# An RGCN layer with a gate on one core: the middle nine weight matrices taken one outer product at a time, each outer product by seven products of quarters

## The chip, the cores and the metric

The kernel runs on one core of a Trainium2 chip. The metric is the device time of one execution in microseconds (us); lower is better. The time of the kernel before is the median of three runs, 1311.46 us (1311.43 to 1313.43).

## The reference

```
h = maximum(layernorm(x), 0)                      # x: 1250 x 1024, float32
u = h @ root + bias
for r in range(8):                                # 20,000 edges (src, dst, type), sorted by dst
    mask = (edge_type == r)
    sums = segment_sum(h[src] * mask[:, None], dst, 1250)
    mean = sums / maximum(segment_sum(mask, dst, 1250), 1)[:, None]
    u = u + mean @ weight[r]                      # weight: 8 x 1024 x 1024
z = concatenate([u, h], 1) @ w_gate + b_gate      # w_gate: 2048 x 1024
out = x + tanh(u) * z + h * (1 - z)
```

Everything is float32. The mean commutes with the product, so the kernel first makes `h @ weight[r]` for all nodes and then gathers rows of it for the edges.

## The kernel before

**Eleven matrices.** `mats` is the eight `weight[r]`, then `root`, then the lower half of `w_gate` (these ten are multiplied by `h`), then the upper half of `w_gate` (multiplied by `u`). The code counts them s = 0 to 10; "matrix six" in this text is s = 5. The 1250 rows of `h` are ten blocks of 128 rows (`ND`, the last of 98), taken in five pairs (`NP`): pair i is the blocks i and i + 5.

**The outer seven products.** One pair (256 rows) times one matrix (1024 x 1024) is done by the Strassen-Winograd scheme: seven products of a 128x512 operand with a 512x512 operand in place of eight. The seven left operands of all pairs are made once and kept in SBUF (`h_op[i]`, slots `A11, A12, A22, S1, S2, S3, S4`); the seven right operands of a matrix (`Factors`) are made by four VectorE subtractions of 128x2048, `make_t1` to `make_t4`, in nine buffers `wbuf`. One 128x512 operand times one 512x512 operand is four matmuls with 512 moving columns (`KQ` = 4, line L509).

**The inner seven products.** For the matrices s = 1 to 9 the two row blocks of two neighbouring pairs (0 and 1, 2 and 3) are taken together for some of the seven kinds of product, and Strassen-Winograd is applied once more: seven products of quarters with 256 moving columns (two matmuls each, line L253 in `Second.add`) in place of eight. The classes `Second`, `Third`, `First` and `Fifth` do this for A12, S4, A11 and S1. The other three kinds, and all seven kinds of the fifth pair, which has no partner, stay at 512 columns. For s = 8 and 9 `Fifth` serves the first two pairs alone (`fifths`). Each class makes its inner sums on VectorE for each two pairs: four 128x512 differences of the right operand and four 128x256 sums of the left operands (`Third.sums` and `next_sums`, L307 to L316). The four 128x256 sums of the left operands for `Second` are made once, at s = 1, kept in DRAM (`lefts_dram`) and loaded again.

**Order of the work.** `steps` runs over (s, i), matrix outside and pair inside. `step` calls `product` for one pair. `product` issues the seven outer products and, in the places that the dictionary `fill` gives, the inner ones. After each of them it calls `between(j)`, which first issues what the matrix itself needs (loads of the next matrix, `make_t1` and so on, inner sums) and then one or more steps of a generator with side work. Engines run their own queues in order, and buffers and semaphores tie them; so the position in the program decides behind what an instruction stands on its engine.

**Results.** PSUM has eight banks here: four `ps`, two `ps_b` (`lead`), `ps_n` and `ps_q`. Products are copied or added from PSUM into two SBUF tiles `row` of 128x1024, and `put` stores each finished block of 512 KB in one transfer from the SP queue to `y[g]`, `hr_dram` or `z_dram`.

**Side work.** At s = 0 the layer norm and the transposes of `h` go on beside the matmuls. The generator `index()` builds a table of the edges: `scatters()` issues 157 small indirect transfers from GpSimd (`to_table`, L1011), each followed by three `memset` of `apart` (L1019), and advances one step for two of them; `order()` loads the table back (`in_table`, L1260, from the SP queue), counts (`of_nodes`, L1024 and on, VectorE), sends the counts through DRAM to all partitions (`v_bc`, L1265), and ranks the nodes (`larger`, L1034). From s = 5 on, the generator `edges` gathers rows of `y[0]` (matrices s = 0 to 4) for 118 slots of edges, from s = 8 on rows of `y[1]` for 75 slots: `add_slot` issues an indirect gather of 128 rows on GpSimd (L1448) and one 128x1024 multiply-add on VectorE (L1453). `spread` divides the steps evenly over the `between` calls. GpSimd runs ahead of VectorE by the five buffers `got`.

**The end.** The gate product (s = 10) is five calls of `product` with `u` as the left operand, with tanh, the mixing and a scatter of the rows to the output.

A part of `step` that shows how the old order is put together (i = 1):

```
fill = dict(first=lambda: (e.first(), q and q.first(t[1][:, :Q]), 0)[-1],
            fifth=lambda: (e.sixth(), True),
            sixth=lambda: (e.seventh(), e.to_first(to), 0)[-1])
```

## Time and profile before

| | |
|---|---|
| median of three runs | 1311.46 us (1311.43 to 1313.43) |
| the profiled execution's own time | 1308.14 us |
| its span, first to last instruction | 1306.4 us |
| granted TensorE clock | 0.998 |
| busy: TensorE, VectorE, GpSimd, ScalarE | 1290.2, 956.8, 632.2, 285.2 us |
| bytes moved | 263.12 MB, mean 201 GB/s |

The profile shows one execution. A float32 matmul of the program stands in the trace as two MATMUL instructions, so counts of matmul instructions are twice those of the code. A group's "busy" is the union of its instructions' times; durations of pipelined instructions overlap, so the distance from start to start is shorter than one duration. "PEld" is the weight loads, "SP" the engine that issues transfers, "POOL" is GpSimd, "DVE" is VectorE, "ACT" is ScalarE.

### The profile page before, as it was taken

To read this page: it belongs to the slowest core of one execution; us is meant where nothing else is said; L and a number is where in the kernel's file an instruction comes from. 1 tells how busy PE (TensorE), PEld (TensorE's weight loads), DVE (VectorE), ACT (ScalarE), POOL (GpSimd) and SP (SyncE) were. 2 spreads that over 40 slices of the span, in tenths; PEclk is the share of its full clock that TensorE was granted. 3 is DMA by queue.
4 is the path that set the end of the run, shared out by engine and by line. 5 is a ranking of instruction groups with operands and counts; after the bars stand their busy time and mean duration, and the time that the engine had idled before them with its cause. 6 is when DMAs were issued, how large, how long until landed. Compare 5 with 4: busy or idle time off the path is not lost.

```text
span 1306.4 us, 13118 instructions
## 1 busy us (share of the span) xinstructions
PE 1290.2 (99%) x4075; PEld 758.7 (58%) x4075; DVE 956.8 (73%) x1439; ACT 285.2 (22%) x530; POOL 632.2 (48%) x974
## 2 busy tenths in 40 slices
PE   9999999999999999999999999999999999999997
PEld 5344666566566656646665665666566466544443
DVE  7964653553454797458998988998888899867974
ACT  3342222122122212212221221222122112122210
POOL 0046666665664057402454546556265555615632
PEclk9999999999999999999999999999999999999999
DMA  8864113311422362445648779788789958979951
GB/s 316 295 192 154 67 76 123 116 49 56 155 85 74 132 123 62 70 148 188 233 151 333 247 252 361 287 295 305 244 276 336 381 157 269 340 248 304 340 159 60
DMA packets 110306, 263.12 MB, mean 201 GB/s; under 512 B 34424, under 2 KB 36021, under 8 KB 110099
## 3 DMA queue, kind: packets, MB, share of 16 engines
q0 software_dynamic: 44064, 118.20, 28.1%
q1 hardware_dynamic: 50034, 112.03, 24.8%
q10 hardware_dynamic: 16128, 31.98, 7.4%
q8 instruction: 32, 0.52, 0.2%
q14 instruction: 48, 0.39, 0.1%
HBM read 200.74 MB, written 76.42 MB: 212 GB/s over the span
## 4 chain that ended last, share of the span: by engine, by line
PE 46%; issue 5%; POOL 2%; DMA 2%; DVE 1%; ACT 0%; POOLq 0%; DVEq 0%
PE ps_b L509 22%; PE ps L253 11%; PE ps L509 3%; PE ps_n L253 2%; PE ps_b L253 2%; PE ps_q L253 2%; PE ps_q L509 2%; PE ps_n L509 2%; DMA got<-y,idx 2%; POOL out_dram L907 1%; POOL got L901 0%; POOL got L1448 0%; PE ps L452 0%; POOL h_op L901 0%; DVE h_op L490 0%
## 5 line engine op out<-in xcount | busy, mean ns | idle before, releaser
L509 PE MATMUL ps_b<-w,h_op 128*128 128x512 f32 x1464 | 657.1, 593 | 2.2 <-ACT row L617 1.6
L509 PEld LDWEIGHTS ps_b<-w,h_op 128*128 128x128 f32 x1464 | 276.6, 190 | 303.7 <-issue 290.6
L1448 POOL DMA_INDIRECT got<-y,idx x193 | 254.4, 1318 | 267.8 <-DVE u L1453 177.5
L1453 DVE SCALAR_TENSOR_TENSOR u<-got,w_of,u 128x1024 f32<-128x1024 f32 (+1 forms) x193 | 247.1, 1283 | 38.0 <-DMA got<-y,idx 35.5
L1011 POOL DMA_INDIRECT table<-row_col,at_i x157 | 171.3, 1091 | 173.3 <-issue 101.2
L509 PE MATMUL ps<-w,h_op 128*128 128x512 f32 (+1 forms) x296 | 129.7, 581 | 2.5 <-DVE h_op L490 1.9
L253 PE MATMUL ps<-inner 128*128 128x256 f32 x480 | 120.8, 380 | 0.6 <-DVE inner L308 0.4
L253 PEld LDWEIGHTS ps<-inner 128*128 128x128 f32 x480 | 91.1, 190 | 26.6 <-issue 10.6
L509 PEld LDWEIGHTS ps<-w,h_op 128*128 128x128 f32 x296 | 56.0, 190 | 69.7 <-issue 64.1
L253 PE MATMUL ps<-w,h_op 128*128 128x256 f32 x352 | 90.3, 379 | 0.0
L253 PEld LDWEIGHTS ps<-w,h_op 128*128 128x128 f32 x352 | 66.8, 190 | 31.1 <-issue 22.4
L535 ACT COPY row<-ps_b 128x512 f32<-128x512 f32 x53 | 31.0, 585 | 231.0 <-PE ps_b L509 227.2
L617 ACT COPY row<-ps_b 128x512 f32<-128x512 f32 x54 | 31.6, 585 | 220.9 <-PE ps_b L509 220.9
L253 PE MATMUL ps<-w,w 128*128 128x256 f32 x288 | 69.8, 379 | 0.0
L253 PEld LDWEIGHTS ps<-w,w 128*128 128x128 f32 x288 | 54.8, 190 | 15.9 <-issue 9.6
L661 ACT COPY row<-ps_b 128x512 f32<-128x512 f32 x40 | 23.4, 585 | 176.6 <-PE ps_b L509 165.2
L1019 POOL MEMSET apart<- 128x1 f32 x471 | 52.6, 112 | 18.1
L949 POOL DMA_INDIRECT node_dram<-ids,pos_i x20 | 26.4, 1318 | 54.7 <-DVE pos_i L1277 48.9
L509 PE MATMUL ps_q<-w,h_op 128*128 128x512 f32 x112 | 51.8, 592 | 0.0
L570 ACT COPY row<-ps_b 128x512 f32<-128x512 f32 x54 | 31.7, 588 | 82.7 <-PE ps_b L509 78.4
L193 DVE TENSOR_TENSOR w<-w,w 128x2048 f32<-128x2048 f32 (+1 forms) x12 | 25.3, 2112 | 29.0 <-PE ps L509 29.0
L541 DVE TENSOR_TENSOR row<-row 128x512 f32<-128x512 f32 x44 | 30.2, 686 | 20.4 <-ACT row L535 20.3
(232 smaller groups left out, 1536.1 us busy)
## 6 DMA issues: line engine op xcount, KB each, us to landing
y<-row SPq DMA_DIRECT2D x72, 512.0 KB, 4.8
w<-in_L_gnn_weight_dram ACTq DMA_DIRECT2D x21, 1024.0 KB, 10.4
w<-in_L_gnn_weight_dram SPq DMA_DIRECT2D x10, 1024.0 KB
w<-lefts_dram SPq DMA_DIRECT2D x16, 512.0 KB, 4.5
w<-in_L_gnn_w_gate_dram ACTq DMA_DIRECT2D x6, 1024.0 KB, 15.6
h_dram<-h_op SPq DMA_DIRECT2D x9, 512.0 KB, 6.4
u<-in_L_gnn_bias_dram SPq DMA_DIRECT2D x9, 512.0 KB
hr_dram<-row SPq DMA_DIRECT2D x9, 512.0 KB, 6.4
```

The source lines that it names most:

```text
L193: nc.vector.tensor_sub(p["t1"][:, k], p["t3"][:, k], p["b11"][:, k])
L253: nc.tensor.matmul(p, a[:, k, :], b[:, k, :], start=(fresh and k == 0), stop=(k == 1), skip_group_check=True)
L509: nc.tensor.matmul(b[:, at], aop[:, i, k, :], w.of[i][:, k, at], start=(fresh and k == 0), stop=(k == KQ - 1), skip_group_check=True)
L535: nc.scalar.copy(d, b)
L541: nc.vector.tensor_add(c22, c if lone else c22, d)
L570: nc.scalar.copy(c11, b)
L617: nc.scalar.copy(c12, b)
L949: ins = nc.gpsimd.indirect_dma_start(out=node_dram[g][:, :], out_offset=bass.IndirectOffsetOnAxis(ap=pos_i[:, g, d:d + 1], axis=0), in_=id ...
L1011: ins = nc.gpsimd.indirect_dma_start(out=table[:, :], out_offset=bass.IndirectOffsetOnAxis(ap=at_i[:, c:c + 1], axis=0), in_=row_col[:, c: ...
L1019: nc.gpsimd.memset(apart, 0.0)
L1448: nc.gpsimd.indirect_dma_start(out=t[:n], out_offset=None, in_=y[g][:, :], in_offset=bass.IndirectOffsetOnAxis(ap=at[:n, d, k:k + 1], axis=0),
L1453: nc.vector.scalar_tensor_tensor(u[:n], t[:n], w, u[:n], op0=OP.mult, op1=OP.add)
```

## The change

For s = 1 to 9 the order is turned round. `steps` now runs over (s, n), where n is one of the seven kinds of outer product in the order A11, A12, S2, S3, S1, S4, A22, and `kind(m, n, between)` does this kind for all five pairs before the next one begins.

- Pairs 0 and 1 form one inner scheme, pairs 2 and 3 another (u = 0, 1). Both share the right-hand differences, which `inner_sums` now makes once for a kind and not once for each two pairs, and the left-hand sums of both lie in one 128x512 operand.
- All seven kinds go by seven products of quarters for s = 1 to 4. From s = 5 on `REGULAR` names kinds that stay at 512 columns and are chained onto what the banks hold: A12 and S4 for s = 5 to 7; A12, S2, S3 and S4 for s = 8 and 9; A22 too for s = 9. The fifth pair stays at 512 columns (`alone`).
- Left-hand sums are kept in DRAM for all seven kinds at s = 1 and loaded for all of them at s = 2 to 4; later for S3 alone, where it isn't regular; else VectorE makes them.
- The four `ps` banks are held through all nine matrices, one for each of the pairs 0 to 3, and each kind accumulates onto them where the scheme allows. `ps_n` and `ps_q` hold the inner partial products.
- Rows leave as halves of 256 KB: `put` notes a store, and `store_rows` issues it on the SP queue one call later. All weight loads go from the SP queue; before, most went from ScalarE's.
- Each kind has five `between` calls. `spread` weighs them by the kind (`SHARE`).
- `to_table` has one `memset` in place of three. `in_table`, the counts and `v_bc` go by GpSimd's queue and not by SP's. `larger` is one for each call.
- The first pair of the gate is prepared during the last two kinds of s = 9 (`hooks`), with its operands in other slots of `h_op`.

The diff, cut to its core:

```
+    REGULAR = ((1, 5), (1, 2, 3, 5))
+    LOADED = (3,)
+    SHARE = (9, 11, 9, 11, 9, 11, 10)
...
+    ORDER = (A11, A12, S2, S3, S1, S4, A22)
...
+    def regular(s, n):
+        return s >= R0[1] and n in REGULAR[s >= R0[2]] or (s, n) == (LAST, 6)
+    def loaded(s, n):
+        return 1 < s < R0[1] or s >= R0[1] and n in LOADED
...
+    def inner_sums(m, n, second):
...
+        if from_dram:
+            nc.sync.dma_start(lefts[:, both], kept)
+        if second:
+            nc.vector.tensor_sub(t3, b22, b12)
+            nc.vector.tensor_sub(t4, b21, t2)
+            if not from_dram:
+                nc.vector.tensor_sub(s3, a11, a21)
+                nc.vector.tensor_sub(s4, a12, s2)
+        else:
+            nc.vector.tensor_sub(t1, b12, b11)
+            nc.vector.tensor_sub(t2, b22, t1)
+            if not from_dram:
+                nc.vector.tensor_add(s1, a21, a22)
+                nc.vector.tensor_sub(s2, s1, a11)
+        if m.s == 1:
+            nc.sync.dma_start(kept, lefts[:, both])
...
+    def kind(m, n, between):
...
+        if chained:
+            alone(range(KQ))
+            alone_rows()
+            call(0)
+            m.make(n)
+            for j, i in enumerate((0, 2, 1, 3)):
+                add(banks[i], h_op[i][:, ORDER[n]], w, fresh=n not in (1, 5))
+                if i == 2:
+                    to_rows_of(0)
+                if i == 0:
+                    next_sums()
+                call(j + 1)
+            to_rows_of(1)
+            return
+        x = sum_bank("ps_n")
+        xs = [x[:, :H], x[:, H:]]
+        for u in range(2):
+            add(xs[u], h_op[2 * u][:, ORDER[n], 0:2], b11, fresh=u == 0)
+        if s == 1 and n == 0:
+            for b in banks:
+                touch(b)
+        for u in range(2):
+            nc.scalar.copy(banks[2 * u][:, :H], xs[u])
+        inner_sums(m, n, 1)
+        y = sum_bank("ps_q")
+        for u in range(2):
+            add(y[:, u * H:(u + 1) * H], left_sum(0)[:, u], right(0), fresh=u == 0)
+        ys = ys_room[n % 2]
+        nc.scalar.copy(ys, y)
+        call(0)
+        for u in range(2):
+            add(xs[u], left_sum(1)[:, u], right(1))
+        for u in range(2):
+            add(banks[2 * u][:, :H], h_op[2 * u][:, ORDER[n], 2:4], b21)
+        for u in range(2):
+            nc.vector.tensor_add(banks[2 * u][:, H:], xs[u], ys[:, u * H:(u + 1) * H])
+        call(1)
+        alone(range(KQ))
+        alone_rows()
+        m.make(n)
+        call(2)
+        for u in range(2):
+            add(xs[u], left_sum(2)[:, u], right(2))
+        for u in range(2):
+            nc.scalar.copy(banks[2 * u + 1].rearrange("p (a n) -> p a n", a=2),
+                           xs[u][:, None, :].to_broadcast([P, 2, H]))
+        next_sums()
+        call(3)
+        for u in range(2):
+            add(banks[2 * u][:, H:], left_sum(3)[:, u], b22)
+        to_rows_of(0)
+        call(4)
+        for u in range(2):
+            add(banks[2 * u + 1][:, :H], h_op[2 * u + 1][:, ORDER[n], 2:4], right(3))
+        for u in range(2):
+            b = banks[2 * u + 1][:, H:]
+            nc.vector.tensor_add(b, b, ys[:, u * H:(u + 1) * H])
+        to_rows_of(1)
...
+    def beside_kind(m, n, k):
...
+        if k != 0 and s < LAST:
+            return
+        if s < LAST:
+            to = {3: "a", 4: "c", 5: "b", 6: "d"}.get(n)
+            if to:
+                matrix_of(s + 1).load(to)
...
@@ to_table
-        for _ in range(3):
-            nc.gpsimd.memset(apart, 0.0)
+        nc.gpsimd.memset(apart, 0.0)
@@ of_nodes
-        nc.sync.dma_start(val_dram.rearrange("g (p d) -> p g d", p=P), val3)
+        nc.gpsimd.dma_start(val_dram.rearrange("g (p d) -> p g d", p=P), val3)
@@ order
-                for _ in range(7):
-                    yield
                 in_table = sp.tile([P, NHI, SLOTS], I32, name="in_table")
-                nc.sync.dma_start(in_table, table.rearrange("(b p s) o -> p b (s o)", p=P, s=SLOTS))
-                for _ in range(8):
+                nc.gpsimd.dma_start(in_table, table.rearrange("(b p s) o -> p b (s o)", p=P, s=SLOTS))
+                for _ in range(14):
                     yield
                 of_nodes(in_table, sp.tile([P, NHI, SLOTS], F32, name="is_edge"), runs, val, ids_f)
                 v_bc = sp.tile([P, G, KEYS], F32, name="v_bc")
-                nc.sync.dma_start(v_bc.rearrange("p g k -> p (g k)"),
+                nc.gpsimd.dma_start(v_bc.rearrange("p g k -> p (g k)"),
                                   val_dram.rearrange("(o g) k -> o (g k)", o=1)
                                   .to_broadcast([P, G * KEYS]))
                 for _ in range(4):
                     yield
...
-                        if d % 2 or at_call[0] == NP - 1:
-                            yield
+                        yield
```

`alone` is the fifth pair's four matmuls of 512 columns; `alone_rows` and `to_rows_of` copy (ScalarE) or add (VectorE) the banks into the half rows and note the stores; `call(k)` issues stores noted earlier, the weight load of `beside_kind` and the side work.

More of the change, by code (lines that the diff above doesn't have):

```diff
@@ new lines, in quarter_rows, with matrix_of @@
+    def quarter_rows():
+        t = [rows.tile([P, D], F32, name="row") for _ in range(4)]
+        q = [r[:, c:c + Q] for r in t for c in (0, Q)] + [b[:, k] for b in halves
+                                                          for k in range(KQ)]
+        sums_of["rows"] = q[:NP], q[NP:2 * NP], q[2 * NP:3 * NP]
+    matrices = {}
+    def matrix_of(s):
+        if s not in matrices:
+            matrices[s] = Matrix(s, matrices[s - 1].w if s > 1 else None)
+        return matrices[s]
+    stores = []
@@ new lines, in store_rows, with put @@
+    def store_rows(n=None):
+        for _ in range(len(stores) if n is None else n):
+            nc.sync.dma_start(*stores.pop(0))
+    def put(s, i, part, half, t):
+        d = i + part * NP
+        n = nrows(d)
+        if s >= ROOT:
+            to, o = (hr_dram, z_dram)[s - ROOT], d * P
+        else:
+            g = max(k for k in range(G) if R0[k] <= s)
+            to, o = y[g], (s - R0[g]) * N + d * P
+        if half is None:
+            nc.sync.dma_start(to[o:o + n, :], t[:n])
+        else:
+            stores.append((to[o:o + n, half * Q:(half + 1) * Q], t[:n]))
@@ L628, in product @@
             p2(a)
-        elif whole and not third:
+        elif not third:
             p3()
@@ L1521, in spread, with kinds @@
             return between
+        def kinds(s, n, last):
+            return [(a, b) for a in range(s, last + 1) for b in range(7) if (a, b) >= (s, n)]
         def passes_needed():
```

753 lines of the change are left out of this document (242 added, 511 removed).

## The prediction

> **What bounds the kernel now.** I read the page's busy times first, then the groups of TensorE by form, then TensorE's timeline inside one matrix, and last the stretches by engine.
>
> ```profile
> span 1306.4 us, 13118 instructions
> ...
> PE 1290.2 (99%) x4075; PEld 758.7 (58%) x4075; DVE 956.8 (73%) x1439; ACT 285.2 (22%) x530; POOL 632.2 (48%) x974
> ```
> ```profile
> L509 PE MATMUL ps_b<-w,h_op 128*128 128x512 f32 x1464 | 657.1, 593 | 2.2 <-ACT row L617 1.6 <-PEq L1720 0.3 <-ACT h_op L459 0.2
> L509 PE MATMUL ps<-w,h_op 128*128 128x512 f32 x280 | 126.1, 593 | 2.5 <-DVE h_op L490 1.9 <-ACT row L591 0.6
> L253 PE MATMUL ps<-inner 128*128 128x256 f32 x480 | 120.8, 380 | 0.6 <-DVE inner L308 0.4 <-DVE top L1547 0.3
> L509 PE MATMUL ps_q<-w,h_op 128*128 128x512 f32 x112 | 51.8, 592 | 0.0
> L509 PE MATMUL ps_n<-w,h_op 128*128 128x512 f32 x96 | 43.2, 592 | 0.0
> ```
>
> TensorE is busy for 99% of the span, and the idle times in front of its matmuls are 2.2, 2.5 and 0.6 us. No other engine ends its waits for more than moments. But "busy" could hide slow matmuls; so the timeline, where a line's start against the next line's start gives the real pace:
>
> ```profile
> 378.41 3.60 PE L509 MATMUL ps_b<-w,h_op 128*128 128x512 f32 x8
> 381.84 0.38 PE L132 MATMUL ps<-ident 128*128 128x512 bf16 x1
> 382.06 1.03 PE L253 MATMUL ps<-inner 128*128 128x256 f32 x4
> 382.92 1.03 PE L253 MATMUL ps_n<-w,inner 128*128 128x256 f32 x4
> 383.80 1.13 PE L253 MATMUL ps<-inner,h_op 128*128 128x256 f32 x4
> 384.76 1.03 PE L253 MATMUL ps_n<-w,h_op 128*128 128x256 f32 x4
> ...
> 393.38 1.89 PE L253 MATMUL ps<-w,w 128*128 128x256 f32 x8
> 395.11 3.17 PE L509 MATMUL ps_b<-w,h_op 128*128 128x512 f32 x7
> ```
>
> Eight matmul instructions of 512 columns take 381.84 - 378.41 = 3.43 us, 0.429 each. Eight of 256 take 395.11 - 393.38 = 1.73, 0.216 each, also from group to group (382.06 to 382.92: 0.86 for four). Half the columns cost half the time, to 0.003 us in two. So the kernel is bound by the number of columns that TensorE streams, and a change is worth the columns that it saves, less the waits that it makes.
>
> **TensorE's part.** I count the program's matmuls as 512-column and 256-column ones. Before: s = 0: 140 and 0; s = 1 to 7: 76 (three kinds of four pairs and seven of the fifth, times 4) and 112 (four classes, two schemes, 14); s = 8 and 9: 84 and 98; s = 10: 136 and 8. That makes 976 and 988. The trace has two instructions for one, and the four groups of L509 with 512 columns have 1464 + 280 + 112 + 96 = 1952 = 2 x 976, so the count holds. After: s = 1 to 4: 28 and 196 (seven kinds of 28); s = 5 to 7: 60 and 140; s = 8: 92 and 84; s = 9: 108 and 56; s = 0 and 10 as before. That makes 768 and 1352. So 208 x 2 = 416 instructions of 0.429 go (178.5 us) and 364 x 2 = 728 of 0.216 come (157.2 us): 21.2 us less. `touch` (L132) was called ten times (once at the start, once for each of the nine matrices) and is called five times now, 0.22 each (381.84 to 382.06): 1.1 less. In sum 22.3 us, all on the path, as TensorE has no idle time to hide them in.
>
> By stage: a kind by quarters lasts 56 x 0.216 + 8 x 0.429 = 15.5 us, a regular one 40 x 0.429 = 17.2. A matrix took 113.6 and takes 108.7 at s = 1 to 4, 111.9 at s = 5 to 7; at s = 8 and 9 it took 114.4 and takes 115.2 and 116.9.
>
> On the price of narrow matmuls the Trainium skill (TensorEngine Tiling (Array Packing), Instruction Overhead) speaks against this change: it gives each matmul some 60 cycles of overhead on TRN2. As an estimate by that page and the 2.4 GHz of TensorE: Matmul & The Clock Gate, 312 more instructions would cost 25 ns each, 7.8 us of the gain. The trace doesn't agree: two instructions of 256 take 3 ns more than one of 512.
>
> **What VectorE must do in the same time.**
>
> ```profile
> 590.00:930.00 340.00, 340.00 (x1121) 210.94 (x1120) 302.09 (x431) 68.95 (x142) 174.38 (x137) 1.00 0.77 268
> 930.00:1160.00 230.00, 229.65 (x732) 137.31 (x731) 195.05 (x253) 46.89 (x93) 124.29 (x95) 1.00 0.83 289
> ```
> ```profile
> L1453 DVE SCALAR_TENSOR_TENSOR u<-got,w_of,u 128x1024 f32<-128x1024 f32 x184 | 235.7, 1283 | 34.8 <-DMA got<-y,idx 32.3
> L310 DVE TENSOR_TENSOR inner<-w,inner 128x512 f32<-128x512 f32 x52 | 35.8, 688 | 3.3 <-PE ps_b L253 3.2
> L205 DVE TENSOR_TENSOR w<-w,w 128x2048 f32<-128x2048 f32 x11 | 25.2, 2290 | 0.0
> L315 DVE TENSOR_TENSOR inner<-h_op,inner 128x256 f32<-128x256 f32 x52 | 21.9, 422 | 0.0
> L384 DVE TENSOR_TENSOR ps_b<-ps,inner 128x256 f32<-128x256 f32 x18 | 7.7, 429 | 9.4 <-PE ps L253 9.4
> ```
>
> The third pair of numbers of a stretch is VectorE: 302.1 of 340 us (89%) at s = 5 to 7. Per matrix, without the gathered rows, it made 45 operations of 512 elements, 46 of 256 and 4 of 2048: 45 x 0.688 + 46 x 0.422 + 4 x 2.29 = 59.5 us. After, at s = 5 to 7: 20 right-hand and 16 left-hand sums, 20 + 3 additions into rows, 59 in all of 512; 20 of 256 in PSUM; 4 of 2048: 40.6 + 8.6 + 9.2 = 58.4. The gathers stay. So the load is the same in 111.9 us as in 113.6, 89 to 90%. By the same counts VectorE gets 8 us less at s = 8, 15 less at s = 9, 2 more at s = 2 to 4 (62 of 108.7 us) and 81 us at s = 1, where it makes and stores all left-hand sums. Nothing in sum; what matters is when each operation is due.
>
> Inside a kind by quarters (0 to 15.5 us) the products come in the order P1 to 1.7, P5 to 3.5, P6 to 5.2, P2 to 6.9, the fifth pair to 10.4, P7 to 12.1, P3 to 13.8, P4 to 15.5. VectorE's additions of `ys` can start at 5.2 and are due at 10.4; t3 and t4 start at about 2 and are due at 10.4; t1, t2 of the next kind can start at 5.2 and are due at 17.2; the rows of banks 0 and 2 can start at 13 and are due at about 18, when ScalarE must have overwritten the banks. Each has 4 us or more, save ScalarE's two copies after P7 (due within 1.7 us):
>
> ```profile
> L437 ACT COPY ps<-ps 128x512 f32<-128x512 f32 x16 | 9.1, 570 | 6.9 <-PE ps L253 6.9
> ```
>
> Two of 0.57 make 1.1 us, so they fit. VectorE's new in-order waits are for P6, for the fifth pair and for P3; behind each stand the side work and the next sums, and TensorE waits for those only if VectorE is over 4 us late. What can make it late is its wait for gathered rows:
>
> ```profile
> DVE u L1453 <- DMA got<-y,idx: 35.5, 26, 4.6
> ```
>
> 26 waits, 35.5 us in all, 4.6 at the longest: hidden now. Below this cost is nothing (TensorE's idle time before is nearly nothing, so there is nothing to win back); above, all 35.5 us could pass through. I take a tenth, 4 us, since one wait rarely exceeds the 4 us of room and the load is that of before.
>
> **Queues.**
>
> ```profile
> w<-in_L_gnn_weight_dram ACTq DMA_DIRECT2D x21, 1024.0 KB, 10.4
> ...
> w<-lefts_dram SPq DMA_DIRECT2D x16, 512.0 KB, 4.5
> ```
>
> On SP all weight loads now stand behind the stores, which wait for VectorE's rows. The tightest load, the one issued in the last kind, has about 22 us until `make(0)` of the next matrix needs it, against 10.4 to land; ScalarE loses the issues, and no one waits for that. A left-hand load of 4.5 us has 12 us; behind a weight load that began 5 us earlier it lands after 10. Some 44 more transfers of 512 KB run at s = 1 to 4, where the core moves, for one, 116 GB/s and not the 268 to 289 of the rows above:
>
> ```profile
> 400.00:500.00 100.00, 100.00 (x328) 61.52 (x328) 76.03 (x124) 18.94 (x38) 32.00 (x45) 1.00 0.45 116
> ```
>
> I cost both at nothing; without this cover a late weight load would stop VectorE and, 4 us later, TensorE.
>
> The sum: the profiled span 1306.4 - 22.3 + 4 = 1288.1 us; the execution's own time is 1.7 us over its span, 1289.8; the median of the runs is 3.3 us over that execution (1311.46 to 1308.14): **1293 us**.
>
> **Rivals.**
>
> *VectorE late at matrices six to eight* (1307 us). By its rows the kind S2 at s = 5 holds 2.8 + 1.7 + 2.3 + 1.4 + 2.8 us and five gathers of 1.28 (6.5), 17.4 us against 15.5; S3 16.5, A22 17.2; the other kinds less than they last. If the surplus isn't caught up, 1.9 + 1.0 + 1.7 = 4.6 us a matrix, 14 in three; with more of the gather waits up to 21, 1314. Against it: durations overlap.
>
> ```profile
> 430.40 0.69 DVE L308 TENSOR_TENSOR inner<-w 128x512 f32<-128x512 f32 x1
> 431.00 0.42 DVE L309 TENSOR_TENSOR inner<-inner,h_op 128x256 f32<-128x256 f32 x1
> ```
>
> From start to start an operation of 0.69 takes 0.60, so S2 needs about 15.7.
>
> *The table comes late* (slower, 1332 us).
>
> ```profile
> 74.53 1.16 POOL L1011 DMA_INDIRECT table<-row_col,at_i  x1 [72.11 <-DVE at_i L1007]
> 75.67 0.45 POOL L1019 MEMSET apart<- 128x1 f32 x3
> ...
> 413.27 0.98 POOL L1011 DMA_INDIRECT table<-row_col,at_i  x1 [0.63 <-issue]
> ```
> ```profile
> 139.36 1.03 PE L253 MATMUL ps<-w,h_op 128*128 128x256 f32 x4
> ```
> ```profile
> 431.94 0.45 DVE L1024 TENSOR_SCALAR is_edge<-in_table 128x560 f32<-128x560 int32 x1
> ```
>
> 157 scatters run from 74.5 to 413.3, 2.17 us each; L1024 read the table at 431.9 without waiting. By the calls, L1024 comes at call 113, 78 calls into s = 1 and on: 139 + 2 x 108.7 + 15.5 + 10 = 382 us, 50 earlier. With two of three `memset` gone (0.30 of 2.17) the last scatter is at 74.5 + 156 x 1.87 = 366, and the load, now on GpSimd, has 16 us. I allow 9 us from the last scatter's start: about 1 for itself, 2.3 to land (below), about 1 to issue the load and 4.5 for it. It fits, narrowly.
>
> ```profile
> table<-row_col,at_i POOLq DMA_INDIRECT x157, 2.3
> ```
>
> If the pace is set by something else (the 0.63 "issue" of each scatter) and stays 2.17, the load lands at about 422, VectorE stops for 40 us with the inner sums behind L1024, and TensorE idles some 40 - 4 = 36, plus 3 for `v_bc` on the same queue: 1293 + 39 = 1332. The gain of 18 us is gone at 15 us of idle time and these 3, that is if the load lands at 401: from a pace of about 2.04 us. For it: nothing here shows the pace with one `memset`. Against: the three stand in GpSimd's own time.
>
> *Narrow matmuls dearer than the mean row* (1301). The group at 383.80 needs 0.96 us for four (0.24 each) and not 0.86. If the 312 instructions that come on top cost 0.024 more each, as these do, 7.5 us are lost. Against it: this group, on operands made just before, is the exception among those above. The page named above would give about the same time. That the change doesn't save its columns isn't a rival: the count follows from the code.
>
> **How the numbers follow.** Forecast 0.62; VectorE late 0.19 (0.16 faster, 0.02 same, 0.01 slower); table late 0.10; narrow matmuls dearer 0.03; something unnamed 0.06 (0.02 same, 0.04 slower). A measurement tells about 0.2%, 2.6 us. Faster 0.62 + 0.16 + 0.03 = 0.81, same 0.04, slower 0.15. The range goes from 1287 (no new wait, and a little of the old idle time saved) to 1314 (VectorE late at its worst); it leaves out the late table and the unnamed, 0.16.
>
> **What would show it.** The matmul instructions of 512 columns would count 1536, those of 256 2704, at 0.429 and 0.216 from start to start, and TensorE's idle time inside would be some 4 us, in front of matmuls that wait for VectorE at s = 5 to 9. VectorE at s = 5 to 7 would be at about 90%. The last scatter would be at about 366 us and L1024 at 382 with no wait. I am wrong if idle time of over 10 us stands in front of TensorE's matmuls, or if the 256-column ones take more than 0.22.

## The result, and the profile after

The changed kernel takes 1418.81 us (median of four, 1409.89 to 1423.72) against 1311.45 us (1309.68 to 1313.43) of the kernel before beside it: ratio 1.0811, 95% interval 1.0748 to 1.0873. It is 8% slower where 1.4% faster was forecast. The profiled execution took 1422.49 us, its span is 1420.7, the granted clock 0.958.

The page of the changed kernel, its busy times and two of its rows of 40 slices (35.5 us each):

```profile
span 1420.7 us, 13511 instructions
...
PE 1288.0 (91%) x4382; PEld 832.0 (59%) x4382; DVE 962.7 (68%) x1351; ACT 248.0 (17%) x452; POOL 597.0 (42%) x663
...
PE   9992343989999998799899999999999999999997
...
PEclk9996767999999999899999999999999999999998
```

TensorE is busy for 91% of a longer span. The hole is in slices 4 to 7 (about 106 to 249 us), with a lower clock in the same slices, and small dents follow up to slice 20. From there on, where the forecast saw its main risk, TensorE is full.

TensorE by stretches after (the columns are stretch, its length, then busy time and count of each engine; PEclk is the third number from the end). Two matrix lengths at the start, the stretches with dents, and s = 5 to 8 with a part of s = 9:

```profile
20.00:140.00 120.00, 93.20 (x223) 40.99 (x222) 67.19 (x114) 41.24 (x48) 54.83 (x95) 0.90 0.57 179
140.00:254.00 114.00, 48.51 (x115) 25.40 (x114) 17.27 (x25) 6.51 (x13) 89.86 (x159) 0.72 0.14 46
...
482.00:597.00 115.00, 102.06 (x410) 79.29 (x409) 80.44 (x131) 18.65 (x40) 33.88 (x32) 0.96 0.55 154
597.00:710.00 113.00, 106.36 (x422) 81.80 (x421) 64.73 (x125) 21.61 (x45) 16.27 (x16) 0.95 0.43 133
710.00:1200.00 490.00, 490.00 (x1677) 318.01 (x1676) 434.47 (x545) 76.31 (x153) 272.08 (x209) 1.00 0.80 276
sum 1180.00, PE 1060.57 PEld 717.24 DVE 793.74 ACT 209.63 POOL 505.80; mean PE 151.51 PEld 102.46 DVE 113.39 ACT 29.95 POOL 72.26
```

The same seven stretches of the kernel before, their sum:

```profile
sum 1180.00, PE 1175.51 PEld 701.15 DVE 866.20 ACT 260.78 POOL 588.94; mean PE 167.93 PEld 100.16 DVE 123.74 ACT 37.25 POOL 84.13
```

From 20 to 1200 us TensorE now idles 119.4 us in place of 4.5. Over the whole spans it idles 132.7 us in place of 16.2 (span less busy time): 116.5 more. The span grew by 114.3. With the 22.3 us that the columns save, 114.3 + 22.3 - 116.5 = 20.1 us are left: TensorE's instructions themselves took longer, as they would at the lower clock behind each gap. The last run below bears the size out: TensorE is busy there for 1266.6 us with the same 4382 matmul instructions, 21.4 less than the 1288.0 here, at a granted clock of 0.995 and not 0.958.

The worst part is at s = 0, where the products are those of the kernel before. The timeline there:

```profile
103.83 3.60 PE L557 MATMUL ps<-w,h_all 128*128 128x512 f32 x8
...
131.39 0.59 ACT L580 COPY row<-ps_b 128x512 f32<-128x512 f32 x1 [16.58 <-remote]
...
132.03 1.22 PE L557 MATMUL ps_b<-w,h_all 128*128 128x512 f32 x1 [24.60 <-ACT row L580]
```

ScalarE is to copy a bank of `ps_b` that TensorE finished before 107.43 us, and has nothing else to do; it starts at 131.39, "remote" being a release that the view ties to no instruction. TensorE waits for that copy 24.60 us, and its first matmul afterwards takes 1.22 us where 0.59 is usual. All three engines are mostly idle in this stretch, and the transfers are few (DMA share 0.14 in the row of 140 to 254 us). Only GpSimd works all the time. Its scatters after:

```profile
145.00 0.98 POOL L808 DMA_INDIRECT table<-row_col,at_i  x1 [0.19 <-issue]
145.94 0.15 POOL L815 MEMSET apart<- 128x1 f32 x1
146.28 0.98 POOL L808 DMA_INDIRECT table<-row_col,at_i  x1 [0.19 <-issue]
```

They follow at 1.28 us. From start to start the median of the 157 is 1.285 us (2.03 before), the mean 1.43 (2.17 before), and the last one starts at 296.1 us, not at 413.3 and not at the forecast 366.

What comes late can be read from the trace's records of semaphore updates, which no view prints. ScalarE's copy waits for one semaphore only, the one that TensorE's matmuls count up. The last matmul into its bank ends at 103.99 us; the update that releases the copy is recorded at 131.37, 27.4 us later and 0.02 us before the copy starts. From 73 to 300 us, 24 of the 45 recorded updates of this semaphore come over 0.5 us after TensorE's latest matmul that updates it had ended, up to 23.9; in the last run below it is none of 128. No update by ScalarE or VectorE comes over 0.5 us late in either. The ends of matmuls are modelled in a trace, but the eight matmuls behind this one, in the first row above, ran at their usual pace.

One more thing differs in the view of transfers from 140 to 200 us, the changed kernel first, then the kernel before:

```profile
table<-row_col,at_i POOLq DMA_INDIRECT x44
```
```profile
table<-row_col,at_i POOLq DMA_INDIRECT x29, 2.2
```

Before, the view has a landing time, from the semaphore records of the transfers; after, most of these records are missing for as long as the scatters run. That alone is no sign of a stall: in the same stretch the landing time is missing too in two runs below that don't stall there (the changed kernel with 280 columns, timed, and the kernel before with 208).

### The profile page after: what moved, and what is told of

It is laid out like the page before. It is cut to its first block, busy times and chain, and to the rows that moved or that the text cites. A ratio compares the mean times of both kernels' runs of the same rounds, so it can differ in the third digit from the quotient of the medians.

```text
span 1420.7 us, 13511 instructions
## 1 busy us (share of the span) xinstructions
PE 1288.0 (91%) x4382; PEld 832.0 (59%) x4382; DVE 962.7 (68%) x1351; ACT 248.0 (17%) x452; POOL 597.0 (42%) x663
## 5 line engine op out<-in xcount | busy, mean ns | idle before, releaser
L304 PE MATMUL ps<-w,h_all 128*128 128x256 f32 (+1 forms) x1248 | 392.3, 463 | 3.6 <-issue 3.6
L304 PEld LDWEIGHTS ps<-w,h_all 128*128 128x128 f32 x1248 | 238.2, 191 | 138.3 <-issue 116.2
L311 PE MATMUL ps_b<-w,h_all 128*128 128x512 f32 x504 | 226.6, 592 | 0.0
L557 PE MATMUL ps_b<-w,h_all 128*128 128x512 f32 x312 | 148.7, 625 | 69.2 <-issue 43.4
L304 PE MATMUL ps_n<-w,w 128*128 128x256 f32 x768 | 185.3, 385 | 19.3 <-issue 14.3
L304 PEld LDWEIGHTS ps_n<-w,w 128*128 128x128 f32 x768 | 146.9, 193 | 63.0 <-issue 33.5
L311 PEld LDWEIGHTS ps_b<-w,h_all 128*128 128x128 f32 x504 | 95.8, 190 | 95.8 <-issue 92.8
L557 PEld LDWEIGHTS ps_b<-w,h_all 128*128 128x128 f32 x312 | 61.5, 201 | 149.1 <-issue 119.4
L304 PE MATMUL ps_q<-w,w 128*128 128x256 f32 x384 | 95.7, 395 | 10.0 <-DVEq L1510 6.3
L304 PEld LDWEIGHTS ps_q<-w,w 128*128 128x128 f32 x384 | 76.0, 198 | 38.3 <-issue 16.5
L304 PE MATMUL ps_n<-w,h_all 128*128 128x256 f32 x384 | 91.8, 382 | 0.3 <-PEq L1510 0.3
L304 PE MATMUL ps<-w,w 128*128 128x256 f32 x384 | 91.4, 381 | 0.0
L304 PEld LDWEIGHTS ps_n<-w,h_all 128*128 128x128 f32 x384 | 73.8, 192 | 15.2 <-issue 4.8
L223 DVE TENSOR_TENSOR w<-w,w 128x2048 f32<-128x2048 f32 x36 | 82.3, 2286 | 0.3
L304 PEld LDWEIGHTS ps<-w,w 128*128 128x128 f32 x384 | 73.6, 192 | 10.2
```

Of the source, the lines that this page charges most:

```text
L223: nc.vector.tensor_sub(w[to], w[a], w[b])
L304: nc.tensor.matmul(p, a[:, k], b[:, k], start=(fresh and k == 0), stop=(k == a.shape[1] - 1), skip_group_check=True)
L311: nc.tensor.matmul(to, h_op[NP - 1][:, ORDER[n], k], w[:, k], start=(fresh and k == 0), stop=(k == KQ - 1), skip_group_check=True)
L557: nc.tensor.matmul(b[:, at], aop[:, i, k, :], w.of[i][:, k, at], start=(fresh and k == 0), stop=(k == KQ - 1), skip_group_check=True)
```

## The experiments

Theory A: scatters at this pace hold up the semaphore updates by which the engines release each other. Rivals: B, the new arrangement (held banks, row halves, more transfers on SP) stalls s = 0 itself; C, the number of GpSimd instructions between two scatters counts, not the time. The first three groups of runs are from one chip each, the fourth from two; the record doesn't name the chip of the two main profiles. "Pace" is the median from start to start of the 157 scatters.

### Pace or arrangement

Three memsets again in the changed kernel:

```
-        nc.gpsimd.memset(apart, 0.0)
+        for _ in range(3):
+            nc.gpsimd.memset(apart, 0.0)
```

> Only edit to the changed kernel: three memsets behind each table scatter instead of one, as before the change. Theory A (the pace of the scatters: at 1.285 us apart instead of 2.03 they hold up the semaphore updates of the other engines, and TensorE and ScalarE are released late): the scatters are again 2.0 to 2.2 us apart and end near 413 us, the gaps of TensorE on L557 during matrix one (24.60, 19.19, 16.23 us and others, some 107 us of lost pace up to 254 us) go to under 10 us. The table then comes 32 us or so after L820 wants it (position near 389 us once the stalls are gone), so VectorE stops there and TensorE with it for up to 36 us. Sum 1419 - 107 + 0 to 36 = 1312 to 1348 us. Theory B (the new arrangement of the products, its row halves and held banks stall matrix one, whatever GpSimd does): gaps as in the changed kernel, 1410 to 1425 us.

Measured: 1335.76 us (the kernel before: 1307.54). The pace is 2.03 us again, the last scatter at 405.2, and no gap is left during the scatters. The table now comes late; VectorE's and TensorE's waits:

```profile
DVE is_edge L821 <- DMA in_table<-table: 29.5, 1, 29.5
```
```profile
PE ps_q L304 <- DVE w L269: 29.1, 2, 27.8
```

One memset in the kernel before:

```
-        for _ in range(3):
-            nc.gpsimd.memset(apart, 0.0)
+        nc.gpsimd.memset(apart, 0.0)
```

> Only edit to the kernel before: one memset behind each table scatter instead of three. Theory A: the scatters go to 1.2 to 1.4 us apart, TensorE gets gaps of 10 to 25 us and the half clock in the stretch from 74 to 290 us, and the time rises by 80 to 110 us, to 1390 to 1420 us. Theory B: the time stays within 3 us of 1311, since the products are the old ones.

Measured: 1309.23 us, no stall, at a pace of 1.284 us. That spoke for B, and was the one run that misled; it is taken up again below.

Three memsets as in the first run, and a later sort:

```
-                for _ in range(14):                  # order
+                for _ in range(24):
...
-            while at_call[1:] != [1, 2]:             # beside_group
+            while at_call[1:] != [2, 2]:
```

> The changed kernel with three memsets behind each table scatter, and with the sort that reads the table placed ten calls (about 31 us) later (24 instead of 14 steps in order; any_over from the third kind on instead of the second, so that it still comes behind the sort). Theory A: no gaps in matrix one, and the table is there when L820 comes, so what is left is the arrangement's own gain of about 22 us less the gaps seen at other places of the changed kernel (the run of twenty indirect DMAs between 574 and 599 us with a gap of 8.95 us, the branch with 6.3 us, 3.7 us beside L830): 1311 - 22 + 10 to 25 = 1299 to 1314 us. Theory B: over 1395 us.

Measured: 1327.08 us, a miss. The table is in time, but the later gathers of `idx` now stand in GpSimd's queue ahead of the zeroing of the tile that the slot counts use:

```profile
DVE got L733 <- POOL got L1216: 28.2, 1, 28.2
```

TensorE lost 21.4 us to it. The later position had moved the sort past something that I hadn't counted.

One wide memset:

```
+    pause = const.tile([P, 280], F32, name="pause")
...
-        nc.gpsimd.memset(apart, 0.0)
+        nc.gpsimd.memset(pause, 0.0)
```

> The changed kernel with its one memset behind each scatter made 280 columns wide, estimated at 0.34 us from the rows of 979 ns for 1024 columns and 135 ns for one: as much GpSimd time as the three narrow ones (3 x 0.112), but one instruction. Theory A, if it is the time between two scatters that counts: pitch near 1.5 us and a good half of the lost 107 us back, 1320 to 1370 us. Theory C (it is the number of instructions between two scatters that gives the others their turn): pitch near 1.5 us, gaps as in the changed kernel, over 1395 us. Theory B: over 1395 us as well.

Measured: 1301.73 us. One instruction of 0.368 us in place of one of 0.135, pace 1.494 us, and TensorE has 110.00 busy us of 110 from 140 to 250 us. The arrangement is the same as in the changed kernel, and so is the number of instructions, which speaks against B and C. It doesn't settle them: the changed kernel as it is didn't run on this chip, and the one run here at 1.284 us didn't stall either. The next two groups settle them, each on a chip that does stall. The expected time for A was too high, since I thought of a matter of degree.

### When it stalls

The wide memset for the first 40 scatters only, then the reverse:

```
-        nc.gpsimd.memset(pause, 0.0)
+        nc.gpsimd.memset(pause if c < 40 else apart, 0.0)
```
```
+        nc.gpsimd.memset(apart if c < 40 else pause, 0.0)
```

> The changed kernel with the wide memset (280 columns, 0.37 us) behind the first 40 table scatters and the narrow one behind the other 117. Known so far: the pace of 1.284 us between scatters costs 107 us in the new arrangement and nothing in the old one (1309.23 us), and at 1.494 us the new arrangement runs without it (1301.73 us). Theory D (a backlog that is set off in the first 50 us, where the scatters meet the loads of matrix two's weights and the transposing transfers, and that then holds itself up as long as the scatters come 1.284 us apart): the start is passed without it, so no gaps afterwards, 1295 to 1308 us. Theory F (at each moment, the fast pace is too much for the new arrangement): gaps on L557 and L304 from about 135 us on, some 76 us of the loss, 1360 to 1400 us.

> The reverse: the narrow memset behind the first 40 table scatters, the wide one behind the other 117. Both theories D and F: gaps up to about 130 us (some 30 us of lost TensorE time in the changed kernel's row up to 140 us), none after, 1325 to 1340 us. If the gaps go on at a pace of 1.49 us, a backlog holds itself up at that pace too, and the time is over 1380 us.

Measured: 1415.80 and 1343.34 us (before: 1310.54). TensorE's busy share follows the pace at each moment; wide then narrow has 116.49 of 120 us from 20 to 140 and 49.10 of 110 from 140 to 250; the reverse:

```profile
20.00:140.00 120.00, 97.45 (x228) 42.90 (x227) 70.91 (x121) 42.17 (x50) 55.68 (x91) 0.90 0.62 190
140.00:250.00 110.00, 110.00 (x419) 79.01 (x418) 65.47 (x102) 20.24 (x42) 98.61 (x135) 1.00 0.38 127
```

So no backlog from the start is needed (theory D falls), and the stall ends when the pause begins. B and C fall with it: within one execution, with one arrangement and one memset behind each scatter, the stall comes and goes with the length of that memset. It is also not tied to the work of s = 0: with the late start of the narrow memset it hits the kinds of s = 1 as hard (the four largest rows of TensorE's waits, 102.5 us in all, are at `L304`).

No memset at all in the kernel before:

```
-        for _ in range(3):
-            nc.gpsimd.memset(apart, 0.0)
```

> The kernel before without any memset behind the table scatters. If the pace has a threshold of its own that the old arrangement only just keeps at 1.284 us, the scatters (1.0 to 1.2 us apart now) bring gaps of 10 to 25 us on L509 in matrix one or two, 1380 to 1430 us. If something that only the new arrangement does is needed, 1305 to 1313 us.

Measured: 1474.17 us. Its row:

```profile
140.00:250.00 110.00, 21.96 (x40) 9.61 (x40) 8.25 (x13) 1.76 (x3) 84.39 (x85) 0.59 0.07 20
```

The old arrangement stalls too, worse than any other run. The pace is again 1.284 us, without a memset as with a narrow one: one narrow memset vanishes in it, and no run has a pace under 1.283.

The loads of matrix two's first two quarters later:

```
-            to = {(2, 3): "a", (3, 3): "c", (NP - 1, 2): "b", (NP - 1, 3): "d"}.get((i, j))
+            to = {(NP - 1, 0): "a", (NP - 1, 1): "c", (NP - 1, 2): "b", (NP - 1, 3): "d"}.get((i, j))
```

> The changed kernel, narrow memset as it is, with the loads of matrix two's first two weight quarters (1 MB each, at 81.64 and 102.51 us) moved to the last row block of matrix one (some 110 us), so that the scatters' first 35 us meet the same transfers as in the kernel before. If these loads set the stalls off: no gaps up to 110 us, and, if the state needs them, none after: 1295 to 1320 us. If not: 1405 to 1425 us as in the changed kernel.

Measured: 1445.48 us, TensorE 90.73 of 120 us from 20 to 140. The transfers that the change adds early don't set the stall off.

### How long the pause, and how sure

The `pause` of 64 columns; that of 280 columns again, timed; one of 208 columns in place of the three in the kernel before; and the kernel before with one narrow memset, timed:

```
-    pause = const.tile([P, 280], F32, name="pause")
+    pause = const.tile([P, 64], F32, name="pause")
```

> The changed kernel with its memset behind each scatter 64 columns wide, estimated at 0.19 us from 0.135 us for one column and 0.368 us for 280. Without a memset in the kernel before, and with the narrow one in both kernels, the scatters come 1.284 us apart at least, so this is the floor of the queue and the narrow memset lies inside it. If any pause that lifts the pitch off that floor is enough, pitch 1.31 to 1.36 us and 1298 to 1310 us. If the pause has to be as long as a waiting engine's turn (some 0.2 us more), gaps stay and the time is 1340 to 1420 us.

> The changed kernel with the 280 columns wide memset once more, timed against the kernel before: 1299 to 1305 us, ratio to the kernel before 0.990 to 0.997, with no gap of TensorE above 2.5 us during the scatters.

> The kernel before with one memset of 208 columns (what its memory leaves room for, estimated at 0.31 us) in place of the three narrow ones. The kernel before has no stall from its table, so a faster table is worth nothing to it: 1308 to 1313 us, within 0.2% of the kernel before. Then what the changed kernel with the wide memset is below it is the new arrangement's own. If it falls to 1300 us or so, the pause is the gain and the arrangement brings nothing.

> The kernel before with one narrow memset, timed in more executions, since it is the one run that speaks against the pace: if the old arrangement really bears the floor pace of 1.284 us, all runs are within 0.3% of the kernel before. If it stands at the edge of the stalled state, some runs are at 1340 us or more.

| kernel | pace, us | time, us (all runs) | ratio to the kernel before |
|---|---|---|---|
| changed, 64 columns | 1.307 | 1432.41 | |
| changed, 280 columns | 1.496 | 1311.46 (1310.12 to 1323.76) | 1.0018 (0.9999 to 1.0037) |
| before, 208 columns | 1.436 | 1313.06 (1312.44 to 1316.42) | 1.0014 (1.0003 to 1.0025) |
| before, one narrow memset | 1.284 | 1420.27 (1418.06 to 1439.65) | 1.0824 (1.0803 to 1.0844) |

The last line settles the main question. The removal of two memsets alone, without the new arrangement, costs 108.7 us (1420.27 - 1311.58); the whole change costs 107.4. The single run of 1309.23 us was on another chip: there the same program at the same pace didn't stall. TensorE's updates are late here too (23 of 45 recorded from 73 to 300 us, up to 23.2 us), and none is in the run of 1309.23 us, nor in the two runs of the table at 1.436 and 1.496 us. The row here:

```profile
140.00:250.00 110.00, 78.95 (x230) 47.20 (x229) 41.69 (x70) 13.77 (x29) 91.38 (x150) 0.84 0.17 56
```

A pause in the old kernel brings nothing by itself (1.0014). But the changed kernel with it is only as fast as the kernel before, where 1299 to 1305 us were expected, so 22 us of the arrangement are missing still. In its timeline stands one more such gap, while GpSimd issues 20 gathers of `idx` and scatters of `node_dram` without a memset, from 459 to 485 us:

```profile
470.16 1.89 PE L304 MATMUL ps_q<-w,w 128*128 128x256 f32 x8
482.23 2.07 PE L304 MATMUL ps_n<-w,w 128*128 128x256 f32 x4 [10.18 <-issue]
```

### Where the arrangement's gain went

A wide memset behind the 40 transfers of this kind too; the same without the branch, that is without the code for nodes with more edges than the table holds and for unsorted edges; and 140 columns behind the table's scatters alone:

```
             tc.add_to_no_dep_group("nodes", ins.ins)
+            nc.gpsimd.memset(pause, 0.0)
...
             rows_of(idx[:, g, d, :], table_rows, node_key[:, g, d:d + 1])
+            nc.gpsimd.memset(pause, 0.0)
```
```
-                counts_over()
```
```
-    pause = const.tile([P, 280], F32, name="pause")
+    pause = const.tile([P, 140], F32, name="pause")
```

> The changed kernel with the wide memset behind the table scatters and also behind each of the 40 indirect DMAs that write node_dram and gather idx. Theory A: the gap of 10.3 us at 471.7 us (with the half clock behind it some 13 us of lost pace, seen in the timed run with the wide memset and absent in the run of 1301.73 us) belongs to the run of twenty such DMAs 1.28 us apart, and goes: 1296 to 1304 us, and the executions lie within 0.4% of each other. If the arrangement itself loses that time there, 1308 to 1313 us as before.

> The same with the branch at matrix five's last kind left out (counts_over: the code for nodes with more edges than the table holds, which this input does not need). The gaps of 5.5 to 6.8 us that TensorE waits for VectorE's sequencer there, and the half clock of some 3 us behind each, go: 8 to 10 us less than the kernel with the branch, 1287 to 1295 us. That would be the gain of the arrangement as forecast (22 us less 4). If the branch's time comes back at the next wait, less than 4 us.

> The changed kernel with the memset behind each scatter 140 columns wide (0.25 us by the durations of 135 ns for one column and 368 ns for 280), pitch estimated at 1.38 us, between 1.307 us (64 columns, 1432.41 us, stalled) and 1.496 us (280 columns, no stall from the scatters). If the edge is the floor of 1.284 us plus a little, no stall, 1300 to 1314 us; if the stalled state needs a pause as long as the wide one to go, 1340 to 1430 us; if it is a matter of degree, between, 1315 to 1360 us.

Measured (one chip, the kernel before 1309.43): 1314.18, 1307.80 and 1304.73 us; ratios 1.0029 (1.0018 to 1.0040), 0.9984 (0.9973 to 0.9996), 0.9972 (0.9956 to 0.9989). The first two are misses. The gap of 10 us is gone, but not shown to be so by the pauses: the third run has none behind these 40 transfers, and TensorE is busy for 30.00 us of 30 from 460 to 490 us in it as well, as it was in the first run with the wide memset. The gap was seen on the chip of the timed run and not on these two. What the pauses did do is make the gathers later, and the wait seen in the run with the later sort came back, VectorE first, then TensorE:

```profile
DVE got L734 <- POOL got L1218: 19.5, 1, 19.5
```
```profile
PE ps_q L304 <- DVE w L269: 13.9, 1, 13.9
PE ps_q L304 <- DVEq L1513: 6.1, 1, 6.1
```

The branch costs 6.4 us between the first two runs, a little less than expected. At 140 columns (pace 1.376) the table's scatters don't stall on this chip.

The pauses of the first of these at 140 columns, with the counts five calls later; and the same without the branch:

```
-    pause = const.tile([P, 280], F32, name="pause")
+    pause = const.tile([P, 140], F32, name="pause")
...
-            while at_call[1:] != [1, 2]:
+            while at_call[1:] != [2, 2]:
```

> The changed kernel with the 140 columns wide memset behind the scatters and behind the 40 indirect DMAs of node_dram and idx, and any_over with the slot counts five calls later ([2, 2] in place of [1, 2]), since in the run with all pauses VectorE stood 19.5 us in the slot counts for the zeroing of got (L1218, GpSimd), which lies in GpSimd's queue behind the last idx gathers, and TensorE 13.9 us for VectorE's sums behind it. Expected: that wait and the gap in the run of twenty DMAs are both gone, 1297 to 1303 us, 0.5 to 0.9% below the kernel before, and the executions closer together than with 140 columns alone (1301.85 to 1311.01). If the wait for got comes back with the later counts: 1305 to 1312 us.

> The same without the branch (counts_over left out): 7 to 10 us less, 1288 to 1295 us, which would be the forecast's 1293.

Measured on a further chip: ratios 1.0288 (1.0246 to 1.0329) and 1.0285 (1.0253 to 1.0318), single runs from 1334.54 to 1366.19 and 1343.62 to 1356.69. VectorE's wait for `got` is gone, but 140 columns don't keep the scatters clear here, at the same 1.376 us:

```profile
140.00:250.00 110.00, 93.17 (x365) 70.61 (x364) 60.06 (x93) 18.29 (x39) 95.96 (x145) 0.95 0.29 98
```

So these two say nothing on the branch; they say that the edge differs from chip to chip. The last run takes a longer pause:

```
+    pause = const.tile([P, 400], F32, name="pause")
...
+            nc.gpsimd.memset(pause[:, :280], 0.0)      # behind each node_dram scatter and idx gather
...
-        nc.gpsimd.memset(apart, 0.0)
+        nc.gpsimd.memset(pause, 0.0)
...
-            while at_call[1:] != [1, 2]:
+            while at_call[1:] != [2, 4]:
```

> The changed kernel with a memset of 400 columns behind each table scatter (pitch estimated at 1.60 us from 1.376 us at 140 and 1.496 us at 280 columns; last scatter near 343 us, L820 near 389 us), 280 columns behind the 40 indirect DMAs of node_dram and idx, and any_over with the counts seven calls later. At 140 columns the stall was absent on one chip (1304.73 us) and present on another (1355.34 us), so this takes a pause that has kept clear on three chips and lengthens it. Expected: no gap of TensorE during the scatters or the runs of twenty, no wait of VectorE for got, the branch still there (6 us and its half clock): 1297 to 1304 us, 0.6 to 1.0% below the kernel before. If a stall remains at a pitch of 1.6 us, the pitch is not the condition: over 1315 us.

Measured: **1294.91 us** (1294.62 to 1295.86), the kernel before 1309.04: ratio 0.9894 (0.9876 to 0.9912). It beats both kernels, on the chip where 140 columns gave 1304.73. Which of its three edits brings that difference isn't separated. Its page, and TensorE's largest waits:

```profile
span 1293.1 us, 13551 instructions
...
PE 1266.6 (98%) x4382; PEld 822.8 (64%) x4382; DVE 963.4 (75%) x1351; ACT 248.0 (19%) x452; POOL 669.1 (52%) x703
...
PEclk9999999999999999999999999999999999999999
```
```profile
PE ps_q L304 <- DVEq L1513: 5.6, 1, 5.6
PE ps L501 <- DVE h_all L890: 2.0, 1, 2.0
PE ps_n L304 <- ACT ps L395: 2.0, 2, 1.6
PE ps L557 <- DVE h_all L539: 1.9, 1, 1.9
PE ps_q L304 <- DMA w<-lefts_dram: 1.4, 1, 1.4
```

## Why the prediction was wrong, step by step

**The step that failed is in the rival of the late table**, where I took two of three memsets away as "0.30 of 2.17" and noted that they "stand in GpSimd's own time". Both halves are wrong. With the memsets went a part of the idle time ahead of the next scatter (0.63 us "issue" became 0.19), so the mean from scatter to scatter fell to 1.43 us (the median to 1.285) and not to 1.87. And the time between two scatters wasn't GpSimd's own: without it TensorE's semaphore updates came late, the one shown above by 27.4 us. The sum had no term for what a faster GpSimd does to the others; I had a chance of 0.10 on the scatters being too slow, and none on their being too fast. The scatters alone cost 108.7 us (the kernel before with one memset).

**The late table itself** was priced well in sum, in part by luck. At the old pace the load did come after L820's place, and that run took 1335.76 us against the rival's 1332. But VectorE waited 29.5 us for it and TensorE 29.1, where the rival had 40 and 39; other waits fill the difference, among them 6.3 us behind the branch (below) and 5.8 for VectorE's additions in PSUM.

**TensorE's columns: right.** The 512-column rows below and their kind sum to 504 + 480 + 312 + 120 + 80 + 40 = 1536 instructions, those of 256 columns to 2704 (first and last of six groups, after):

```profile
L311 PE MATMUL ps_b<-w,h_all 128*128 128x512 f32 x504 | 226.6, 592 | 0.0
...
L557 PE MATMUL ps_q<-w,h_all 128*128 128x512 f32 x40 | 18.0, 592 | 0.0
```

The pace of the narrow ones is 0.216, as in the timed run with 280 columns, eight from start to start in 1.73 us:

```profile
463.25 1.89 PE L304 MATMUL ps_n<-w,w 128*128 128x256 f32 x8
464.98 1.89 PE L304 MATMUL ps<-w,w 128*128 128x256 f32 x8
```

So the rival of dear narrow matmuls falls. The 60 cycles for each matmul that the prediction cites from the Trainium skill (TensorEngine Tiling (Array Packing), Instruction Overhead) don't show here as a charge on every instruction: two of 256 columns take 3 ns more than one of 512.

**The sum: right in size, once the pauses are there.** The last run's span is 1293.1; before it was 1306.4. By the views of waits TensorE waits 16.6 us in it (nine rows) and 7.8 in the kernel before (nine rows), 8.8 more; 1306.4 - 22.3 + 8.8 = 1292.9. The forecast had 4 us for new waits, so its span of 1288.1 was 5 us short, and named the wrong ones.

**Gathered rows and VectorE at s = 5 to 7: the allowance of 4 us was not needed.** Even the changed kernel as it is has 490.00 busy us of 490 from 710 to 1200 us, with VectorE at 434.47 (89%, as forecast for s = 5 to 7). The rival of 0.19 falls.

**Queues costed at nothing: wrong by small sums.** The left-hand loads on SP cost TensorE up to 4.0 us in the runs without a stall (1.4 in the last rows above, 4.0 with pauses everywhere). GpSimd's zeroing of `got` behind the gathers, which the text didn't name, cost TensorE 13.9 us with pauses everywhere and 21.4 in the run with the later sort. A wait that I hadn't looked for at all is the branch (L1510): VectorE stops there in the changed kernel,

```profile
688.78 0.68 DVE L359 TENSOR_TENSOR w<-w,ps 128x512 f32<-128x512 f32 x1
696.49 0.69 DVE L263 TENSOR_TENSOR w<-w 128x512 f32<-128x512 f32 x1 [7.02 <-DVEq L1510]
```

and TensorE 5.5 to 6.7 us behind it, as the next kind's sums come from VectorE; in the kernel before VectorE stood 4.3 us at its branch, and TensorE 0.3.

**What stays open.** Shown, for both arrangements and between runs of one chip, is that scatters at 1.284 to 1.307 us stall the kernel, that a longer pause between them ends the stall, and that TensorE's updates come late while it lasts. By what path the transfers hold them up is not shown.

Nor is it known whether the recording of an execution takes part, and that rival is a strong one. In all the runs of the second and third group, in the two with 140 columns and later counts, and in the changed kernel, 126 to 207 of some 2,300 to 2,500 updates by TensorE, ScalarE and VectorE have no record, in the runs without a stall too (156 with 280 columns, timed). In the other runs of the first and fourth group, and in the kernel before, hardly any is missing. So every stall on record goes with a trace that loses records, and no trace that keeps them has a stall. Every execution on record has a span and a clock, which come from a recording, so there is none without one to compare. What sets those chips apart, why one chip bears 1.284 us and another not 1.376, is open, and so is how the changed kernel as it is would run on a chip that keeps its records. The 400 columns ran on one chip only, and not on the one where 140 stalled.

## What to carry to other kernels

An instruction that does nothing may be a pause that other engines live on: before a "useless" one on GpSimd is removed, look at what its queue does without it, and at the other engines' idle time marked "remote" or "issue" after. A transfer queue that runs at its shortest distance (here 1.284 us) for long is a warning by itself; space it, and test the spacing on more than one chip. Judge an edit by runs of one chip on which the fault has been seen: two steps here, the first wide memset and the pauses behind the gathers, ran where nothing stalled and so showed less than they seemed to. When work moves to a later place, list what lies ahead of it in each in-order queue, and control flow too: the two smaller losses here were of that kind.

## What was not expected of the hardware

- Indirect scatters of 128 four-byte rows from GpSimd follow each other at 1.284 us, with no memset or with a narrow one between (medians; the shortest distance of all is 1.280); 280 columns give 1.494 us, 400 give 1.593. Kernels at 1.28 to 1.31 us throughout took 1410 to 1474 us, with one exception on one chip (1309.23); at 1.376 us one chip stalled and one didn't; at 1.436 us and above no profile shows a stall during the table's scatters.
- What comes late in the stall is TensorE's semaphore updates, one by 27.4 us in the changed kernel; of ScalarE's and VectorE's recorded ones none is over 0.5 us late. The Trainium skill (SBUF — State Buffer, Who interferes with whom) names only VectorE and GpSimd as engines that block each other in SBUF, and says of TensorE and ScalarE that they never wait on anyone. Here ScalarE stood 16.58 us before a copy from PSUM with its input ready; that rule speaks of SBUF and doesn't cover it.
- A gap costs more than its length: behind 24.60 us of idle time the 512-column matmul took 1.22 us and not 0.59, and the clock granted from 140 to 254 us was 0.72. By the Trainium skill (TensorE: Matmul & The Clock Gate, Part 1: The HAM clock gate (the "warmup" mystery)) the array falls to half its clock after an idle window of some 3.4 us and needs about as long of work to come back. The 1.22 us, about twice 0.59, agrees with the half; the 3.4 us no run here measures.
- A branch that isn't taken goes with 7.02 us of standstill of VectorE in the changed kernel; without it, the run with pauses everywhere is 6.4 us shorter.
